# Two graph layers on one core: operations written in the order of their places, a new opening, and new places for the first and last graphs

## The chip, the cores and the metric

The kernel runs on one core of one Trainium2 chip. The metric is the device time of one execution in microseconds (us), as the median of several runs. The engines of the core are called PE (TensorE, matrix products; PEld is its loading of weights), DVE (VectorE), ACT (ScalarE), POOL (GpSimd) and SP (SyncE, which here only issues DMAs).

## The reference

There are 64 graphs of 256 nodes with 512 features each, and a weighted adjacency `adj` of 256 x 256 per graph. Two layers follow each other; each normalizes its input, applies a graph operation and adds the result to its input.

```python
# layer 0
h = jnp.maximum(_layernorm(x), 0.0)
deg = jnp.sum(adj, axis=-1, keepdims=True)
agg = jnp.einsum('bij,bjf->bif', adj, h) / jnp.maximum(deg, 1e-6)
x = x + relu(jnp.einsum('bnf,of->bno', jnp.concatenate([h, agg], axis=2), W))
# layer 1
h = jnp.maximum(_layernorm(x), 0.0)
Xw = h @ Wv + bv
sj, si = Xw @ aw[:512, 0], Xw @ aw[512:, 0]
e = leaky_relu(sj[:, None, :] + si[:, :, None] + ab[0], negative_slope=0.2)
alpha = adj * jnp.exp(e)
transition = alpha / (jnp.sum(alpha, axis=-1, keepdims=True) + 1e-12)
H, Xk = 0, h
for k in range(3):
    H = H + Xk @ Wk[k] + bk[k]
    Xk = jnp.einsum('bij,bjd->bid', transition, Xk)
x = x + relu(H)
```

## The kernel before

All products are float32. The kernel does fewer of them than the formula has: blocks of the two factors are added and subtracted first, so that seven block products do the work of eight (and 26 those of 32 for `W`), and the results are combined while they come out of PSUM. The sums of left and right factors are made by POOL and DVE, PSUM is emptied by ACT and DVE, and PE multiplies. PSUM has eight banks, `bank[0]` to `bank[7]`.

**Stages of one graph.** `prepare` (layernorm, Relu, degree scaling), `wide` (the 26 products with W, from tables `EARLY` for graphs 0 and 1 and `STEPS` for the others), `layer0` (the product with the scaled adjacency, in `main`, and the residual in `finish`), `turn1` (second layernorm and the four row sums that give `sj` and `si`), `transition` (the softmax-like matrix), `moved`, `once` (transition times h), `inner` (what is multiplied by the transition a second time) and `outer` (the three terms summed, in `main` again, and the store). Several graphs are in flight at once: while `outer` of one graph runs, `wide` and `layer0` of the next ones fill its gaps.

**Turning matrices.** For most graphs a matrix is transposed by DVE in blocks of 32 (`put`), written to DRAM by four DMAs (`dh`, `dan`, `dtt`) and read back (`get`). The first graphs and the last two, where nothing hides the trip, are transposed by PE instead (`flip_on_pe`, tagged L404 in the profile). `sj` also goes through DRAM: one DMA writes it (`ds<-sj`), a second one (`row<-ds`) reads it back onto all partitions; `transition` then applies Prelu and Exp to it on ACT (L692, L695), weights it with the adjacency on DVE (L697), scales it on ACT (L703, `an`) and has it transposed (`tt`).

**The weights.** At the start `weights_l0` loads the four half-megabyte blocks of W into the buffers of later x tiles (L784), PE transposes them in eight groups of four 128 x 128 blocks (L796), ACT copies them out, and DVE forms the right-hand sums from them (28 operations, L812 and L814). `weights_l1` does the same for the second layer's weights.

**What sets the order.** Nothing is scheduled automatically. `Plan.add` records each operation with its engine, its reads and writes and a *place*: a number from the table `AT`, plus the graph's number times `TURN`. `Plan.emit` sorts the operations of each engine by place; that is the engine's order in the program. It then writes the engines' queues into one program, so that nothing is written ahead of what it depends on: engine by engine, as far along each queue as possible. The tables whose names end in `_0`, `_1`, `_2` hold the places of graphs 0 to 2, those in `_late` and `_last` those of graphs 62 and 63, and `first` and `weights` those of the opening; the other tables serve all graphs between.

**DMA semaphores.** DMAs take eight completion semaphores in turn, in the order in which they are written into the program, and an issue waits until the previous user of its semaphore has landed. So at most eight DMAs are in flight, and SP, which issues in order, stands still at the ninth until the first has landed.

**Names that the change touches.** `first` (the opening loads), `warm` (dummy products; `WARM` is 0 before, so there are none), `main` with its branch `last` for graph 63 (banks `p, r, d` and two spare banks 6 and 7), `AT`, and the ACT costs in `norm_relu` and `scaled`, which are only noted, not executed. In `main`, steps 5, 1, 6 and 7 accumulate one after the other in bank `p`; after each, DVE adds a seed to what stands there into another bank, on which steps 2, 3 and 4 continue.

Of the kernel before, what the change touches and what calls it, by code (L numbers as in the profile page):

```python
# [15 lines left out]
P = 128  # L16
# [8 lines left out]
WARM = 0  # L25
TURN = 38.52
AT = {
    "first": (-90.93, -53.23, -117.99, -108.94, -110.36, -116.23, -69.23, -51.75, -160.39, -107.21, -61.21, -22.37, -27.53, -12.34, -45.26, -1.78,
        -84.29, -28.27, -93.32, 13.37, -47.15, -20.43, -156.60, -71.50, -119.21, -46.84, -42.27, -129.45, -122.63, -61.71, -52.35, -32.94, -72.67,
        -62.56, -45.91, -151.57, -67.52, -60.72, 2.83, 15.02, -11.78, 19.40, 29.16, -47.95, -25.77, 48.23, -47.81, -32.81, -19.46, -48.89, 7.13,  # L30
        20.41, -32.63, 17.85, 10.53, -123.51, 5.76, 21.86),
    "inner": (105.13, 108.59, 106.23, 109.69, 109.89, 110.76, 112.05, 116.38, 111.97, 114.07, 117.47, 117.50, 122.79, 115.08, 117.06, 118.02, 137.51),
    "inner_0": (104.64, 107.10, 112.63, 109.63, 108.85, 109.21, 114.17, 115.99, 113.73, 110.41, 129.80, 114.72, 119.54, 110.75, 113.34, 116.02,
        129.11),
    "inner_1": (110.70, 112.22, 111.49, 112.47, 113.83, 115.31, 114.08, 115.66, 116.33, 115.18, 129.29, 117.74, 125.91, 116.89, 117.80, 117.56,
        155.03),
    "inner_2": (110.70, 111.20, 111.98, 113.63, 111.78, 114.32, 114.94, 116.88, 115.46, 116.06, 116.42, 116.98, 124.86, 117.74, 119.04, 117.57,
        134.35),
    "inner_last": (336.53, 367.29, 384.59, 334.45, 391.73, 454.67, 522.64, 533.37, 408.60, 470.37, 504.02, 528.93, 492.30, 558.54, 500.07, 537.12,
        580.23),  # L40
    "inner_late": (108.31, 111.76, 110.85, 113.85, 112.13, 112.69, 114.05, 114.68, 123.33, 115.61, 145.82, 118.27, 122.89, 115.88, 119.11, 120.04,
        164.89),
    "layer0": (20.96, 24.01, 34.26, 38.15, 36.30, 37.47, 38.90, 39.56, 40.20, 40.90, 41.49, 42.16, 41.93, 42.79, 43.22, 43.47, 44.25),
    "layer0_0": (43.30, 43.73, 40.76, 63.15, 62.04, 64.91, 63.69, 65.17, 65.45, 66.86, 68.03, 68.37, 68.31, 69.19, 69.32, 68.45, 68.75),
    "layer0_1": (31.27, 36.57, 33.97, 43.43, 46.13, 48.74, 46.62, 49.21, 46.86, 49.66, 48.01, 49.83, 48.25, 48.79, 50.67, 49.93, 50.78),
    "layer0_2": (24.88, 28.19, 23.22, 43.47, 37.98, 37.09, 39.47, 39.22, 40.19, 41.59, 40.57, 42.04, 42.75, 43.10, 41.23, 47.00, 44.33),
    "layer0_last": (50.01, 57.68, 33.91, 60.79, 65.66, 66.71, 68.41, 66.94, 69.01, 68.24, 69.91, 69.27, 70.80, 71.03, 72.73, 71.96, 75.23),
    "layer0_late": (15.20, 21.71, 35.30, 40.31, 42.84, 48.47, 47.89, 49.57, 47.98, 49.76, 48.90, 49.94, 48.91, 50.48, 49.70, 51.70, 50.97),
    "loads": (-59.49, -45.29),
    "loads_2": (-40.12, -36.06),  # L50
    "loads_last": (-58.91, -32.90),
    "loads_late": (-54.89, -85.13),
    "moved": (89.04, 92.46, 93.17, 93.66, 94.15, 98.50),
    "moved_0": (94.08, 96.00, 97.15, 96.58),
    "moved_1": (87.63, 93.34, 94.62, 96.56, 97.69, 105.10),
    "moved_2": (88.68, 91.56, 91.23, 91.84, 96.02, 106.19),
    "moved_last": (139.05, 163.46, 205.96, 169.91),
    "moved_late": (96.66, 97.72, 100.63, 101.15),
    "once": (61.25, 64.00, 75.09, 75.88, 94.29, 95.59, 94.96, 99.41, 98.19, 98.63, 100.80, 101.23, 101.56, 100.30, 105.75, 103.00, 102.97, 103.89,
        106.56, 107.35, 108.14),  # L60
    "once_0": (85.34, 86.38, 98.69, 87.50, 93.62, 98.46, 98.58, 97.73, 98.58, 100.34, 100.69, 102.20, 101.36, 98.56, 103.24, 103.33, 102.27, 102.98,
        104.33, 105.25, 108.42),
    "once_1": (57.59, 69.48, 97.24, 96.50, 95.31, 95.58, 95.01, 99.66, 97.26, 98.27, 100.29, 102.15, 100.46, 102.80, 103.34, 105.40, 106.15, 108.95,
        105.21, 110.88, 111.17),
    "once_2": (63.41, 76.25, 69.81, 96.68, 93.52, 97.13, 93.09, 100.30, 100.95, 102.43, 103.05, 103.30, 102.21, 102.90, 103.59, 109.13, 104.57,
        107.39, 107.54, 109.97, 115.46),
    "once_last": (102.80, 135.83, 148.28, 162.89, 124.41, 120.18, 145.98, 187.50, 162.35, 203.89, 212.10, 233.57, 187.89, 213.05, 223.02, 232.11,
        256.18, 243.42, 255.25, 267.18, 321.27),
    "once_late": (66.99, 88.23, 64.29, 90.92, 99.96, 101.37, 100.45, 101.19, 101.37, 101.90, 105.80, 107.13, 110.31, 103.81, 110.60, 107.37, 105.93,
        106.50, 106.70, 107.63, 115.35),  # L70
    "outer": (108.93, 110.52, 122.87, 129.37, 114.22, 117.68, 119.41, 120.07, 120.70, 121.57, 122.87, 123.53, 124.60, 125.46, 126.33, 126.99, 127.62,
        130.65, 131.52, 132.19, 128.92, 131.95, 134.55, 134.99, 141.93, 152.31, 138.02, 140.19, 162.69, 160.60, 164.14, 164.93),
    "outer_0": (94.35, 98.74, 125.62, 106.70, 102.31, 116.27, 117.12, 118.24, 117.50, 117.80, 121.31, 124.46, 124.00, 125.58, 126.52, 126.71, 128.22,
        128.87, 132.65, 133.67, 128.80, 131.21, 134.36, 137.61, 140.55, 144.44, 136.33, 141.49, 160.49, 160.36, 163.66, 166.03),
    "outer_1": (106.89, 111.90, 118.77, 120.53, 108.75, 117.68, 119.18, 119.21, 120.59, 120.95, 123.23, 122.93, 123.75, 126.63, 126.70, 127.43,
        127.87, 128.74, 130.19, 132.33, 130.44, 131.84, 139.05, 141.13, 148.79, 152.10, 133.45, 136.68, 160.29, 160.80, 164.22, 166.72),
    "outer_2": (108.39, 111.96, 127.91, 140.81, 108.40, 121.23, 123.19, 121.63, 124.71, 125.64, 126.27, 125.65, 128.28, 128.68, 129.01, 128.91,
        131.04, 134.92, 135.36, 134.36, 132.23, 135.69, 137.94, 142.17, 143.69, 152.32, 138.41, 140.22, 150.30, 161.80, 164.00, 171.57),
    "outer_last": (498.02, 668.57, 694.33, 671.17, 577.46, 581.61, 593.26, 565.87, 615.19, 623.17, 650.49, 630.60, 695.13, 726.44, 735.87, 784.68,
        743.01, 838.42, 843.34, 796.04, 842.17, 761.60, 792.50, 751.08, 788.70, 811.00, 818.37, 858.45, 840.44, 876.17, 953.80, 975.74, 975.14,  # L80
        1020.56, 876.63, 891.60, 907.44, 875.80, 872.80),
    "outer_late": (109.06, 117.31, 186.73, 151.51, 116.15, 116.30, 119.62, 120.47, 120.01, 120.90, 123.12, 123.38, 129.10, 132.52, 132.66, 129.78,
        134.77, 139.77, 140.44, 139.50, 141.87, 144.49, 145.13, 158.57, 188.07, 200.85, 150.49, 152.04, 158.47, 232.29, 199.18, 211.96),
    "prepare": (-43.06, -41.74, -40.72, -35.30, -36.24, -28.72, -27.19, -23.45, -19.80, -15.93, -24.36, -24.98, -20.94, -12.75, -1.76, -2.28, -14.82,
        -13.49, -12.68, -12.13, -11.03, -11.58, -0.32, 1.04, 0.48, 2.14, 1.59),
    "prepare_0": (-84.88, -53.30, -37.93, -28.72, -22.39, -78.13, -74.85, -6.63, -18.20, -7.49, -144.71, -60.68, -137.04, -101.76, -12.58, -21.22,
        -26.38, -2.11, -10.47, 18.05),
    "prepare_1": (-15.07, -17.62, -8.06, -6.13, -0.14, -1.19, -0.63, 0.54, 7.75, 18.63, -38.44, -18.61, -14.54, 4.73, 16.46, 7.28, 12.55, 17.02,
        21.02, 19.33),
    "prepare_2": (-29.75, -29.48, -28.24, -24.75, -27.62, -28.40, -18.19, -16.40, -14.88, -13.91, -13.33, -6.35, -3.17, 8.62, 7.51, 7.67, -7.58,  # L90
        -2.32, -3.08, -1.25, 10.97, -0.12, 9.45, 9.24, 6.13),
    "prepare_last": (-41.49, -47.42, -40.82, -36.74, -38.40, -39.37, -36.21, -27.41, -24.96, -22.93, -7.95, -5.29, -3.53, 0.52, -2.38, -0.41, -8.95,
        -8.06, 0.10, 9.16, 6.05, -3.83, 2.64, 1.68, 2.00, -1.88, -3.02),
    "prepare_late": (-34.61, -47.32, -24.01, -19.75, -22.44, -22.19, -20.22, -19.93, -12.10, -16.22, -28.31, -35.76, -26.99, -25.62, -0.63, -19.64,
        -11.10, -13.45, -13.43, -9.03, -11.19, -7.53, -0.35, -0.68, -1.43, -1.97, 0.33),
    "prepared": (-7.18, 5.89, 11.28),
    "prepared_0": (8.94, 11.22, 28.01, 44.28),
    "prepared_1": (30.89, 31.47, 31.46, 30.86),
    "prepared_2": (13.00, 25.59),
    "prepared_last": (9.25, 6.90, 2.69),  # L100
    "prepared_late": (-3.13, 0.63, 10.23),
    "transition": (52.39, 56.28, 64.51, 63.42, 65.05, 63.97, 66.52, 67.12, 67.73, 68.04, 68.40, 68.92, 69.51, 71.25, 71.80, 70.70, 72.35),
    "transition_0": (74.09, 74.94, 85.61, 86.74, 87.55, 87.22, 90.49, 90.24, 90.60, 91.41, 91.25, 92.03, 91.61, 91.53, 93.51, 94.10),
    "transition_1": (53.67, 62.32, 65.20, 65.85, 69.15, 70.70, 67.77, 67.85, 67.92, 69.48, 74.55, 74.24, 70.13, 70.67, 70.52, 71.81, 77.46),
    "transition_2": (50.97, 58.93, 62.74, 64.48, 64.38, 64.92, 66.27, 66.53, 66.87, 67.29, 67.28, 69.70, 68.73, 73.40, 72.79, 67.23, 74.57),
    "transition_last": (75.67, 87.14, 127.84, 118.12, 129.35, 119.80, 108.57, 101.56, 114.50, 118.16, 130.61, 133.55, 117.50, 129.78, 119.38, 136.82),
# [165 lines left out]
def gnn_two_layers(ctx: ExitStack, tc: tile.TileContext, x, adj, w0, wv, bv, aw, ab, wk, bk, out):  # L272
# [628 lines left out]
    def first():  # L901
# [7 lines left out]
        weights_l0()  # L909
        load(0, "a")  # L910
        load(1, "x")
        load(1, "a")

    def warm():

# [60 lines left out]
```

## Time and profile before

| | before |
|---|---|
| median of 3 runs | 2546.91 us (2546.01 to 2550.6) |
| the profiled execution's own time | 2545.75 us |
| its span in the profile | 2544.0 us |
| granted TensorE clock, mean | 0.997 |
| PE busy | 2509.1 us (99%) |
| PEld, DVE, ACT, POOL busy | 2213.5, 1653.6, 1322.6, 1560.1 us |
| bytes moved | 296.85 MB, mean 117 GB/s |

The span is what the instruction records cover; the execution's own time is 1.75 us longer. PE's busy share counts a matrix product as busy from its start to its modelled end, at whatever clock it ran, so "busy" does not mean "at full speed". A float32 product of 128 x 128 by 128 x 256 has two records, a transpose of a 128 x 128 block has one. In the timeline, a row merges equal instructions that follow each other: start, time covered, engine, line, operation, tile written, tile read, shapes, count, and in brackets the idle time ahead of it with what ended that.

### The profile page before, as it was taken

The page shows a single profiled execution, that of the slowest core. Times are in us where ns is not written, and L with a number is a line of the kernel's source. Part 1 is how long each engine was busy: PE and PEld are TensorE (multiplying, and loading weights), DVE is VectorE, ACT ScalarE, POOL GpSimd, SP SyncE. Part 2 cuts the span into 40 slices and gives each one's busy share as a digit, 9 for nine tenths or more (in the row PEclk, how much of TensorE's full clock was granted, in tenths as well). Part 3 has the DMA queues.
Part 4 walks back from the last instruction along what each step waited for, and adds up shares of the span by engine and source line. Part 5 has one row for each costly group of instructions (what it writes and reads, how often), then busy time and mean ns, then how long its engine had stood idle before and what let it go on. Part 6 is the DMA issues. An engine that isn't in the chain of part 4 may idle for free.

```text
span 2544.0 us, 39950 instructions
## 1 busy us (share of the span) xinstructions
PE 2509.1 (99%) x12412; PEld 2213.5 (87%) x12412; DVE 1653.6 (65%) x4099; ACT 1322.6 (52%) x3551; POOL 1560.1 (61%) x2475
## 2 busy tenths in 40 slices
PE   7899999999999999999999999999999999999998
PEld 5688888888888888888888888888888888888887
DVE  5766666666666666666666666666666666666654
ACT  7455555555555555555555555555555555555521
POOL 5565666666666666666666656656666666666640
PEclk9999999999999999999999999999999999999999
DMA  4354454454454454444444544544544544544421
GB/s 150 85 131 117 113 129 120 115 125 117 117 129 112 115 135 110 119 125 120 120 120 116 127 121 111 128 122 113 127 119 117 126 113 116 135 112 115 110 71 44
DMA packets 574571, 296.85 MB, mean 117 GB/s; under 512 B 417171, under 2 KB 540819, under 8 KB 574358
## 3 DMA queue, kind: packets, MB, share of 16 engines
q1 hardware_dynamic: 574358, 294.31, 47.0%
q8 instruction: 98, 1.61, 0.3%
q14 instruction: 115, 0.94, 0.1%
HBM read 162.80 MB, written 131.40 MB: 116 GB/s over the span
## 4 chain that ended last, share of the span: by engine, by line
PE 96%; DVE 1%; DMA 1%; SPq 0%; ACT 0%; issue 0%; POOL 0%; DVEq 0%; ACTq 0%; POOLq 0%
PE bank L459 96%; DMA dh<-turned 0%; DMA x<-in_L_gnn_W_dram 0%; DMA l<-in_L_gnn_Wv_dram 0%; SPq L380 0%; DVE bank L474 0%; DVE zg L420 0%; DMA out_dram<-x 0%; DVE z L677 0%; DVE turned L376 0%; PE bank L404 0%; ACT h1n L362 0%; DVE bank L652 0%; SPq L345 0%; DVE zg L474 0%
## 5 line engine op out<-in xcount | busy, mean ns | idle before, releaser
L459 PE MATMUL bank<-l,s 128*128 128x256 f32 x3292 | 876.9, 380 | 6.6 <-ACT bank L546 2.1
L459 PEld LDWEIGHTS bank<-l,s 128*128 128x128 f32 x3292 | 611.6, 191 | 91.4 <-issue 5.1
L471 ACT COPY stg<-bank 128x256 f32<-128x256 f32 x944 | 337.2, 371 | 524.8 <-PE bank L459 203.6
L459 PE MATMUL bank<-l,zg 128*128 128x256 f32 x1820 | 469.2, 380 | 1.6 <-ACT mz L471 0.9
L459 PE MATMUL bank<-lq,zg 128*128 128x256 f32 x1792 | 447.8, 380 | 3.7 <-DVE zg L474 1.3
L459 PEld LDWEIGHTS bank<-lq,zg 128*128 128x128 f32 x1792 | 340.4, 190 | 51.1 <-DVE zg L474 2.3
L459 PEld LDWEIGHTS bank<-l,zg 128*128 128x128 f32 x1820 | 337.2, 191 | 42.3 <-ACT mz L471 1.7
L422 POOL TENSOR_TENSOR zg<-zg 128x256 f32<-128x256 f32 x183 | 131.7, 733 | 353.8 <-ACT zg L471 347.4
L652 DVE TENSOR_TENSOR bank<-bank,stg 128x256 f32<-128x256 f32 x505 | 210.3, 428 | 202.1 <-PE bank L459 138.8
L459 PE MATMUL bank<-l,h0t 128*128 128x256 f32 x1008 | 291.3, 382 | 1.6 <-DVE q L652 0.8
L422 POOL TENSOR_TENSOR s<-h0t,s 128x256 f32<-128x256 f32 x315 | 234.0, 743 | 0.5
L459 PEld LDWEIGHTS bank<-l,h0t 128*128 128x128 f32 x1008 | 197.4, 197 | 26.8 <-DVE q L652 2.3
L677 DVE SCALAR_TENSOR_TENSOR z<-h1n,v_sb 128x512 f32<-128x512 f32 x256 | 211.9, 828 | 13.1 <-ACT h1n L368 4.4
L459 PE MATMUL bank<-l,h1t 128*128 128x256 f32 x784 | 203.3, 381 | 1.3 <-DVE lo L477 1.0
L471 ACT COPY qf<-bank 128x256 f32<-128x256 f32 x128 | 47.6, 372 | 285.3 <-DVE qf L474 250.3
L422 POOL TENSOR_TENSOR qf<-qf 128x256 f32<-128x256 f32 x122 | 113.5, 930 | 117.4 <-DVE qf L474 117.4
L459 PEld LDWEIGHTS bank<-l,h1t 128*128 128x128 f32 x784 | 153.1, 197 | 20.1 <-DVE lo L477 2.3
L563 DVE SCALAR_TENSOR_TENSOR x<-bank,x 128x512 f32<-128x512 f32 x254 | 165.4, 686 | 2.7 <-PE bank L459 1.9
L459 PE MATMUL bank<-q,sa 128*128 128x256 f32 x512 | 152.9, 380 | 2.3 <-DVE bank L474 1.6
L459 PE MATMUL bank<-qf,st 128*128 128x256 f32 x512 | 152.6, 380 | 0.8 <-DVE qf L420 0.7
L422 POOL TENSOR_TENSOR s<-h0t 128x256 f32<-128x256 f32 x189 | 143.5, 773 | 9.3 <-ACT h0t L410 6.6
L422 POOL TENSOR_TENSOR hf<-h1n,hf 128x256 f32<-128x256 f32 x124 | 91.3, 736 | 89.9 <-PE bank L459 89.9
(178 smaller groups left out, 4418.3 us busy)
## 6 DMA issues: line engine op xcount, KB each, us to landing
dh<-turned SPq DMA_DIRECT2D x500, 128.0 KB, 3.3
h1t<-dh SPq DMA_DIRECT2D x64, 512.0 KB, 3.8
x<-in_x_dram SPq DMA_DIRECT2D x63, 512.0 KB, 4.6
out_dram<-x SPq DMA_DIRECT2D x63, 512.0 KB, 3.1
h0t<-dh SPq DMA_DIRECT2D x61, 512.0 KB, 4.0
a<-in_adj_dram SPq DMA_DIRECT2D x64, 256.0 KB, 4.3
dan<-turneda SPq DMA_DIRECT2D x248, 64.0 KB, 1.9
raw<-dan SPq DMA_DIRECT2D x62, 256.0 KB, 2.7
```

Of the source, the lines that this page charges most:

```text
L422: add("POOL", cost, lambda: getattr(nc.gpsimd, f)(to, p, q), reads, writes)
L459: nc.tensor.matmul(ps, lhs, rhs, start=start, stop=True, skip_group_check=True)
L471: add("ACT", 0.37, lambda: nc.scalar.copy(dst, bank[b][:, cols]), [f"bank{b}"], dkeys)
L563: add("DVE", 0.75 if sums else 0.69, lambda c=c: nc.vector.scalar_tensor_tensor(t[:, c, :], bank[banks[1 + c]], 0.0, t[:, c, :], op0=ALU.m ...
L652: add("DVE", 0.43, lambda f=f, to=to, x=x, y=y: getattr(nc.vector, f)(to, x, y), pbk + [k], tok)
L677: add("DVE", 0.79, lambda s=s, c=c: nc.vector.scalar_tensor_tensor(scr.rearrange("p c n -> p (c n)"), h[:, c, :], 1.0, v_sb[:, s, :], op0= ...
```

## The change

1. **Emission.** `emit` writes, of all operations that are ready, the one with the smallest place, one at a time; before, it took engine after engine. Each engine's own order is still the order of its places.
2. **The opening.** The two halves of graph 0's x are issued by ACT, not by SP. Seven groups of four products of the identity with itself go to PE (28 in all, into bank 2): five groups ahead of W0's first blocks and two between its third and fourth group. SP's first issues become: x of graph 1, the four W blocks, adj of graph 0, then bk, adj of graphs 2 and 1 and the weights of layer 1. Before they were: a W block, adj of graph 0, a W block, half of x, a W block, the other half of x, the last W block, then the weights of layer 1.
3. **The last graph.** In the `last` branch of `main`, step 6's sum goes straight to `bank[7]`, where step 3 continues; before it went to the upper half of `bank[r]`, from where ACT copied it to `bank[7]`. That copy (L546) is gone.
4. **Places.** New tables for the opening, for graphs 0 to 2 and for graphs 62 and 63. In the tables of the graphs between, a single number changes (a copy in `inner`, 117.47 to 117.62), which changes no engine's order.
5. Three noted costs of ACT instructions change; no instruction does.

In the two programs' instruction lists, PE's order is the same, and every instruction waits for the same instructions, from about the 520th to the 5910th of PE's some 6270 instructions, and over the matching stretch on the other engines. What differs lies ahead of and behind that: in the profile before, up to about 115 us and from about 2400 us.

```diff
-WARM = 0
+WARM = 7
 AT = {
+    "warm": (-428.00, -428.00, -428.00, -428.00, -428.00, -302.00, -302.00),
...
@@ Plan.emit
-            for e, queue in queues.items():
-                while heads[e] < len(queue) and self.ops[queue[heads[e]]][2] <= done:
-                    i = queue[heads[e]]
-                    self.ops[i][1]()
-                    done.add(i)
-                    heads[e] += 1
-                    left -= 1
+            ready = [(self.ops[q[heads[e]]][3], e) for e, q in queues.items() if heads[e] < len(q) and self.ops[q[heads[e]]][2] <= done]
+            if ready:
+                e = min(ready)[1]
+                i = queues[e][heads[e]]
+                self.ops[i][1]()
+                done.add(i)
+                heads[e] += 1
+                left -= 1
...
@@ main
         p, r, d = banks[:3]
+        e, cols = (banks[4], lo) if last else (r, hi)
...
-        plus(bank[r][:, hi], [f"bank{r}"], p, lo, s12, keys[1:])
+        plus(bank[e][:, cols], [f"bank{e}"], p, lo, s12, keys[1:])
         step(7, p, lo, terms)
         if last:
-            x, y = banks[3:]
+            x = banks[3]
             plus(bank[x][:, lo], [f"bank{x}"], p, lo, s21[:, 1], keys[1:])
             last(1, hi, x, lo)
             plus(bank[d][:, lo], [f"bank{d}"], p, lo, s21[:, 0], keys[:1])
             step(2, r, lo, terms)
-            add("ACT", 0.37, lambda: nc.scalar.copy(bank[y][:, lo], bank[r][:, hi]), [f"bank{r}"], [f"bank{y}"])
             last(0, lo, r, lo)
-            step(3, y, lo, terms)
-            last(0, hi, y, lo)
+            step(3, e, cols, terms)
+            last(0, hi, e, cols)
             step(4, d, lo, terms)
             last(1, lo, d, lo)
...
@@ warm, first
+    def warm():
+        for _ in range(WARM):
+            def run():
+                for k in range(FC):
+                    nc.tensor.matmul(bank[2][:, k * P : (k + 1) * P], ident, ident, start=True, stop=True, skip_group_check=True)
+            add("PE", 0.86, run, ["ident"], ["bank2"])
...
         for c in range(NC):
-            add("SP", 0.8, lambda c=c: nc.sync.dma_start(t[:, c, :], x[0, c * P : (c + 1) * P, :]), [], [f"{k}.{c}"], 3.0, port=256)
+            add("ACT", 0.1, lambda c=c: nc.scalar.dma_start(t[:, c, :], x[0, c * P : (c + 1) * P, :]), [], [f"{k}.{c}"], 3.0)
...
+        kept = plan.count
+        plan.stage("warm")
+        warm()
+        plan.stage("first")
+        plan.count = kept
         weights_l0()
         load(0, "a")
         load(1, "x")
         load(1, "a")
```

## The prediction

> **What bounds the kernel now.** The page first: busy shares (first line) and the forty slices.
>
> ```profile
> PE 2509.1 (99%) x12412; PEld 2213.5 (87%) x12412; DVE 1653.6 (65%) x4099; ACT 1322.6 (52%) x3551; POOL 1560.1 (61%) x2475
> ...
> PE   7899999999999999999999999999999999999998
> ```
>
> PE is the bound; only the outer slices have gaps. Second, the windows by stage (span, time, busy time of PE, PEld, DVE, ACT, POOL, then granted clock, DMA share, GB/s).
>
> ```profile
> 0.00:20.00 20.00, 9.95 (x45) 8.29 (x46) 7.35 (x23) 12.97 (x37) 3.13 (x14) 1.00 0.95 314
> 60.00:80.00 20.00, 14.65 (x59) 9.89 (x57) 14.15 (x35) 13.05 (x38) 15.70 (x25) 0.95 0.33 60
> 80.00:100.00 20.00, 15.23 (x66) 11.79 (x65) 14.34 (x38) 9.10 (x25) 9.74 (x13) 0.80 0.48 112
> 600.00:1000.00 400.00, 400.00 (x1990) 356.31 (x1989) 262.13 (x649) 211.68 (x570) 257.74 (x409) 1.00 0.49 120
> 2520.00:2544.00 24.00, 16.92 (x66) 13.09 (x65) 4.41 (x11) 0.73 (x2) 0.00 (x0) 0.93 0.07 22
> ```
>
> From 600 to 1000 us PE never waits. The instruction lists agree there, so **the change acts only at head and tail**. Idle understates their loss, because PE also runs slowly after gaps. So I count the *excess*: elapsed time less PE's records at their mid-run price (0.2165 us for 128x256, 0.109 for 128x128). It is 15.4 us by 20.6, 19.5 by 41, 27.0 by 70, 38.6 by 91.5, 44.0 by 113, then flat. At the end, idle is 2.7 us in 2400–2520 and 7.1 in 2520–2544, the last store's flight included.
>
> Third, the chain of waits: 96% PE, with W's DMAs, `dh` and a few DVE and ACT lines in the rest. So I went to the timelines of head and tail.
>
> **What the skill says.** "TensorE: Matmul & The Clock Gate", Part 1: PE starts at half clock, gets the full one after some 3.4 us of sustained work and loses it after an idle window as long. The trace agrees in kind: opening transposes take 4.32/19 = 0.227 us against 0.109 later, and after gaps four 128x256 records take 1.92 us, not 1.03. "DMA: Bandwidth & Descriptors", section "Issuing engines are not separate DMA queues": DMAs of ACT and SP share the same 16 engines; a second issuer saves only issue time. Agreed so far as the trace goes: DMA share 0.95 in the first 20 us, an SP issue about 0.43. "ScalarE: Activation LUTs", "What ACT_TABLE_LOAD costs", puts it at 1283 ns; the trace has 1.28.
>
> **Part 1, the opening: -1.9 (bounds -3.5 and +4.8).** PE's timeline (start, time covered, operation, tiles, count, idle before):
>
> ```profile
> 4.35 0.45 PE L796 MATMUL bank<-ident,x 128*128 128x128 f32 x1 [4.35 <-DMA x<-in_L_gnn_W_dram]
> 7.14 2.82 PE L796 MATMUL bank<-ident,x 128*128 128x128 f32 x12 [2.34 <-DMA x<-in_L_gnn_W_dram]
> 11.08 4.32 PE L796 MATMUL bank<-ident,x 128*128 128x128 f32 x19 [1.12 <-DMA x<-in_L_gnn_W_dram]
> ```
>
> PE waits for W, and each transpose runs at half clock. Landings, from the waits: W blocks at 4.32, 7.1, about 9 and 11.03. Issue order gives 0.52 MB by 4.32 and 2.88 by 11.03: 2.36/6.71 = 0.35 MB/us. Queued ahead of W's end after: x of graphs 0 and 1, then W: 2.1 MB by the second block, (2.10-0.52)/0.35 + 4.32 = 8.8 us; 3.15 MB by the last, 11.8. adj of graph 0, second before, lands at about 12.5, not 4.98: its sum on ACT (0.61, L573) now holds the Relu of `h0n` behind it, and DVE's degree operations stand ahead of the sums of W. ACT's two issues (0.43 each) come ahead of its table load (1.28), which then ends near 2.9, before x lands. Wv's second half, on whose landing (19.54) the first W products waited, lands near 18.8.
>
> The 28 unit products have two records each: 0.45 us cold, 0.22 warm (twice the transposes above). Twenty fit ahead of 8.8 us: cold 9 us from 1.3, so up to 10.3. If they bring the full clock, 16 transposes after the last landing take 16 x 0.109 = 1.75, end 13.5 against 15.40 before: **-1.9**. If all stays cold, 28 x 0.45 + 32 x 0.225 = 19.8 from about 0.4 after the identity: ends at 20.2, **+4.8**. I take the warm case: these are plain products, 20 in a row for over 3.4 us. The gain is kept only if `h0n` and the 28 DVE sums (0.34 each, to 25.7 before) move forward as well; -3.5 if Wv's earlier half helps too.
>
> **Part 2, transition of graph 0: -5.5 (bounds 0 and -8.5).** SP's issues, two ACT rows, then PE's:
>
> ```profile
> 57.78 0.35 SPq L686 DMA_DIRECT2D ds<-sj  x1
> 63.50 0.35 SPq L380 DMA_DIRECT2D dh<-turned  x1
> 63.94 0.44 SPq L687 DMA_DIRECT2D row<-ds  x1
> ```
>
> ```profile
> 74.76 0.72 ACT L362 ACTIVATE h1n<-x,sm 128x512 f32<-128x512 f32 x1
> 76.99 0.49 ACT L703 ACTIVATE an<-z,tot 128x256 f32<-128x256 f32 x1
> ```
>
> ```profile
> 77.53 0.44 PE L404 MATMUL bank<-ident,an 128*128 128x128 f32 x2 [0.74 <-ACT an L703]
> 79.62 0.69 PE L404 MATMUL bank<-ident,an 128*128 128x128 f32 x2 [1.65 <-ACT an L703]
> 80.77 1.22 PE L459 MATMUL bank<-tt,h1n 128*128 128x128 f32 x4 [0.46 <-ACT tt L410]
> 81.78 1.92 PE L459 MATMUL bank<-l,s 128*128 128x256 f32 x4
> 85.31 1.19 PE L459 MATMUL bank<-l,s 128*128 128x256 f32 x2 [1.61 <-ACT stg L471]
> ```
>
> `sj` leaves at 57.78, but its read-back is issued 6 us later, behind a `dh` write that waits for DVE. Prelu starts at 68.77, DVE's L697 at 74.41 behind layer 0 of graph 1, and the two `an` scalings come at 76.99 and 79.08 among graph 1's norm (L362, L570, L368). PE has meanwhile run out of layer 0, and flips and products with `tt` follow one by one. From 74.9 to 88.0, 13.1 us pass for 3.5 us of work: 1.04+0.74+1.65+0.46+1.61 = 5.5 idle, the remaining 4.1 slow records.
>
> After: `row` follows `ds` on SP, the two row totals of L700 stand among the additions of layer 0, both `an` stand ahead of graph 1's norm on ACT (some 2.4 us sooner for the first, 4 for the second), and W products of graph 1 and 2 stand between the products with `lq`, `tt` and `st`. I estimate that the 5.5 idle goes and that slow records stay at other, new gaps; all of 1.65+1.04+1.61+slow 4.1 = 8.5 is the far bound, nothing the near one. Next late would be `h1t`, back from DRAM (POOL waits for it 9.55 us at 89.2), and POOL's sums with `hf`. What is moved behind: graph 1's norm, by two `an` (1 us), hidden by W products.
>
> **Part 3, the rest of the ramp: 0 (bounds -5 and +3).** 41–70 lost 7.5 us, 88–113 about 6. Every table of graphs 0 to 2 is new, SP and POOL queues too; no view prices this, so I take nothing: 2 us of `dh` queueing either way is plausible. Issue counts stay, but for two moved to ACT.
>
> **Part 4, the tail: -4.2 (bounds -2.1 and -4.6).** All engines:
>
> ```profile
> 2532.44 0.76 DVE L474 TENSOR_TENSOR bank<-bank,lo 128x256 f32<-128x256 f32 x2 [4.74 <-PE bank L459]
> 2533.24 0.75 DVE L756 SCALAR_TENSOR_TENSOR x<-bank,x 128x256 f32<-128x256 f32 x2
> ...
> 2534.08 0.36 ACT L546 COPY bank<-bank 128x256 f32<-128x256 f32 x1 [13.70 <-DVE x L756]
> ...
> 2534.49 1.13 PE L459 MATMUL bank<-l,s 128*128 128x256 f32 x4 [2.09 <-ACT bank L546]
> ```
>
> Step 7 ends in bank `p`, DVE adds, ACT copies, PE stands 2.09 us, then does 20 records in 6.29 us that cost 4.33 at full clock. After, step 7 precedes step 2, whose 10 records (2.17 us) cover DVE's three operations (0.42+0.34+0.34), and step 3 reads bank 7 directly. From step 7's start, 2527.85, PE has 40 records: 40 x 0.2165 = 8.66, end 2536.5 against 2540.76: **-4.2**. If the clock still drops: 2.09 alone, -2.1. Behind it one DVE operation and the store stay, 3.2 us. Earlier in graphs 62 and 63 flips have fewer fillers: 0 (±0.6).
>
> **Part 5, emission and noted costs: 0.** Waits and order between are identical; at the edges it only decides which queue takes which semaphore, in part 3's bounds.
>
> Sum: -1.9 - 5.5 + 0 - 4.2 = **-11.6**. Against the profiled execution's own 2545.75: 2534.15. The median shown lies 1.16 higher, so **2535.3**.
>
> **Rivals.**
> - A, the sum holds: 0.52.
> - B, the ramp gives part 2 back: DRAM trips of `h1t` (over 9 us of POOL's waiting) set graph 0's pace whatever the transition does. -6.1, 2541: 0.20. For: seven of eight stages wait on them. Against: W products can fill.
> - C, the ramp gains in full (part 2 -8.5, part 3 -3): -17.6, 2529: 0.12.
> - D, the change does not warm: the clock ignores the unit products, +4.8 for -1.9; with the others -4.9, 2542: 0.06. For: the early clock column reads 1.00 while transposes ran cold, so it is no witness.
> - E, slower: Prelu (L692) now stands early in ACT's in-order queue. `row` took 4.83 us, 63.94 to 68.77; ACT's PSUM copies stand behind Prelu, and PE stalls when no bank is free. It decides if `row` lands over about 3 us after Prelu's place; then 3–6 us of stall per graph, doubled by the clock, at graphs 0 and 1: +18 against -11.6, so +6, 2553: 0.10.
>
> **How the numbers follow.** A measurement can tell 0.2% (5.1 us) from none. A and C are faster almost wholly, B for 0.6 of it, D for half: 0.51+0.12+0.12+0.03 = 0.78. Within 0.2%: rest of A, B and D, 0.12; E 0.10. The range, 2527 to 2544, holds A, B, D and most of C, and leaves out E and C's far end. Its ends stand for -20 and -3.
>
> **What would show it.** Right: opening transposes near 0.11 us and W0 done by 14; `row` issued within 1 us of `ds`; no idle over 1 us between 70 and 90, and PE excess 36 or less by 113; the tail's PE gap gone, PE's end 3.2 us ahead of the last landing. Wrong: PE waiting on `h1t`, `row` or Prelu in the 40–110 windows, or transposes at 0.225 until 20 us.

## The result, and the profile after

The changed kernel takes 2534.65 us (2533.68 to 2535.09), before in the same comparison 2548.26 (2546.01 to 2550.6): ratio 0.9946, 95% interval 0.9933 to 0.9959. The forecast was 2535.3, range 2527 to 2544. By these medians 13.6 us are gained; the profiled executions differ by 11.3. The profiled execution took 2534.47 us, its span is 2532.7 (before 2545.75 and 2544.0).

The page again, busy shares and slices: PE has 99% as before, and only its first slices differ.

```profile
PE 2505.8 (99%) x12468; PEld 2212.1 (87%) x12468; DVE 1646.5 (65%) x4099; ACT 1322.9 (52%) x3550; POOL 1562.3 (62%) x2475
...
PE   8899999999999999999999999999999999999998
```

The windows of head and tail (same columns as before; the last one is again the last 24 us of the span):

```profile
0.00:20.00 20.00, 13.65 (x96) 12.96 (x97) 6.38 (x20) 10.88 (x31) 2.04 (x11) 0.95 0.93 328
60.00:80.00 20.00, 15.61 (x71) 10.98 (x70) 17.00 (x48) 15.39 (x45) 14.59 (x25) 1.00 0.30 56
80.00:100.00 20.00, 17.36 (x84) 13.84 (x83) 14.06 (x42) 11.04 (x31) 12.50 (x17) 1.00 0.75 181
2508.70:2532.70 24.00, 18.84 (x84) 15.41 (x82) 6.03 (x15) 0.74 (x2) 2.63 (x4) 1.00 0.07 23
```

PE does 84 records in 80–100 us where it did 66, at clock 1.00 where it was 0.80, and 84 in the last 24 us where it did 66. The first window's 96 records contain the 56 of the unit products, so there is no gain to be read from it.

Both traces have PE's records in full, so record n of before (counted from 0) can be set beside record n + 56 of after. How much earlier PE starts the same ordinal:

| record of before (its time) | after earlier by, us |
|---|---|
| 50th (21.5 us) | -0.8 |
| 100th (31.6) | -1.6 |
| 200th (55.7) | 0.0 |
| 250th (72.1) | 2.0 |
| 300th (90.3) | 8.0 |
| 350th (105.4) | 9.9 |
| 450th (127.5) | 7.1 |
| 1100th to 11700th (258 to 2386) | 7.9 |
| 12380th (2529.65) | 7.4 |
| 12411th, the last (2540.4) | 11.5 |

Up to the 933rd record (224 us in before, not only the 115 us given with the change) and from the 11709th (2388 us) the orders of the two kernels differ, so an ordinal there isn't always the same product, and the split between neighbouring lines is rough; between the two it is the same product. So the opening gives nothing by itself, the stretch of graph 0's transition (250th to 300th) gives 6.0 of the head's 7.9 us, nothing happens for 2100 us, and the last 31 records give 4.0.

The stretch 78 to 88 us shows what kind of gain it was. Before, then after:

```profile
78.00:88.20 10.20, 6.51 (x21) 5.06 (x22) 8.01 (x21) 3.94 (x9) 1.68 (x3) 0.50 0.36 100
```

```profile
78.00:88.20 10.20, 8.78 (x49) 7.35 (x50) 7.16 (x22) 4.87 (x14) 5.60 (x7) 1.00 0.55 121
```

The clock column is 0.50 against 1.00: PE ran the whole 10.2 us at half clock before and at full clock after. Its 6.51 us of records would have taken about half of that by the estimate that every record halves, so some 3.3 us went to the clock alone, beside the idle time. In the whole trace of before half clock stands for 17.1 us (3.4 from 19.9, 10.2 from 78.0, 3.4 from 2535.6), in that of after for 3.4 (from 17.9); the cold start of the opening, where the column reads 1.00, is not in these sums. As half clock can cost at most half of its length, these stretches explain at most 6.9 of the 11.5 us by which PE's last record comes earlier.

### The profile page after: what moved, and what is told of

Same layout as the page of the kernel before. It is cut to its first block, busy times and chain, and to the rows that moved or that the text cites. A ratio compares the mean times of both kernels' runs of the same rounds, so it can differ in the third digit from the quotient of the medians.

```text
span 2532.7 us, 40078 instructions
## 1 busy us (share of the span) xinstructions
PE 2505.8 (99%) x12468; PEld 2212.1 (87%) x12468; DVE 1646.5 (65%) x4099; ACT 1322.9 (52%) x3550; POOL 1562.3 (62%) x2475
## 4 chain that ended last, share of the span: by engine, by line
PE 96%; POOL 1%; DMA 1%; DVE 1%; ACT 1%; issue 0%; SPq 0%; DVEq 0%; POOLq 0%; ACTq 0%
PE bank L462 95%; DMA dtt<-turneda 0%; POOL s L425 0%; DMA x<-in_L_gnn_W_dram 0%; DMA raw<-dtt 0%; DMA raw<-dan 0%; POOL zg L425 0%; PE bank L799 0%; POOL sa L425 0%; POOL hf L425 0%; PE bank L407 0%; DVE bank L477 0%; ACT h1n L365 0%; ACT h1n L371 0%; POOL q L425 0%
```

## Experiments: head, tail, and a stall that had two keys

Each line of the table was timed in five rounds (tail_only, copy_gone, row_early and emit_inner in 11 to 21 executions); "before" is the kernel before in the same comparison. The changed kernel was timed in the first comparison alone. An interval is some 0.13% either way (3.3 us) where before and variant have only those rounds, so differences of 1 to 3 us between variants are read from their traces, by the same alignment of records as above, and not from the medians alone. The profiled execution of before, 2545.75 us, is some 1 to 2 us faster than its medians here, so gains read against its trace are on the small side.

| kernel | us | before, us | ratio (95%) |
|---|---|---|---|
| head_only | 2533.13 | 2547.85 | 0.9942 (0.9929–0.9954) |
| tail_only | 2545.81 | 2547.85 | 0.9991 (0.9983–0.9999) |
| no_warm | 2533.49 | 2547.85 | 0.9945 (0.9931–0.9958) |
| copy_gone | 2544.60 | 2547.85 | 0.9987 (0.9981–0.9994) |
| emit_only | 2562.04 | 2547.34 | 1.0061 (1.0049–1.0074) |
| emit_inner | 2541.50 | 2547.66 | 0.9975 (0.9966–0.9984) |
| row_late | 2537.32 | 2547.34 | 0.9960 (0.9947–0.9972) |
| row_early | 2547.85 | 2547.34 | 1.0001 (0.9993–1.0010) |
| an_late | 2536.48 | 2547.34 | 0.9961 (0.9947–0.9974) |
| undo_trans | 2537.51 | 2546.83 | 0.9966 (0.9952–0.9979) |
| x_on_sp | 2536.24 | 2547.66 | 0.9956 (0.9943–0.9968) |
| opening2 | 2531.15 | 2547.66 | 0.9938 (0.9924–0.9951) |

**head_only**: the changed kernel with before's tables of graphs 62 and 63 and before's `last` branch.

```diff
-    "outer_last", "inner_late", ... : of the changed kernel
+    "outer_last", "inner_late", ... : of before (all names in _last and _late)
-            e, cols = (banks[4], lo) if last else (r, hi)
+            add("ACT", 0.37, lambda: nc.scalar.copy(bank[y][:, lo], bank[r][:, hi]), ...)
```

> The changed kernel with the tail of before: tables of graphs 62 and 63 and the last branch of main with its copy. Theory 1 (the two ends are independent, since the stretch between waits for nothing): the gain of the head alone, 7.7 us by the alignment of the two traces at PE's middle records, so about 3.6 us slower than the changed kernel. Theory 2 (the head's gain is only a shift that the tail's loads and DMAs use): clearly less than 7 us, and head and tail alone do not add up to the whole.

Both theories fell: with the old tail the kernel was not slower than the changed one, and by its trace 1.7 us faster. Its last 31 records gain 4.0 us although the copy is there. The reason stands in its tail, all engines:

```profile
2521.79 1.03 PE L412 MATMUL bank<-l,zg 128*128 128x256 f32 x4
2522.04 0.36 ACT L499 COPY bank<-bank 128x256 f32<-128x256 f32 x1 [12.07 <-PE bank L412]
...
2523.09 1.03 PE L412 MATMUL bank<-l,s 128*128 128x256 f32 x4
2523.29 0.76 DVE L427 TENSOR_TENSOR bank<-bank,lo 128x256 f32<-128x256 f32 x2 [4.74 <-PE bank L412]
```

The copy (L499 here) starts under the products of step 7 and waits for PE alone. In before it started behind DVE's `x` addition (its bracket, shown above, says so), though it needs nothing from that. Both only read the same bank. The tail's new places, on the other hand, cost: from the 11700th to the 12380th record the changed kernel loses 0.5 us where this one gains 0.8.

**tail_only**: before with the other kernel's tail.

```diff
+    all tables in _last and _late, and the branch last of main, from the changed kernel
```

> Before with the tail of the changed kernel: its tables for graphs 62 and 63 and its last branch without the copy; the head and the emission are those of before. Theory 1: 3.6 us faster than before (4.0 in the last graph, 0.4 lost ahead of it), PE's gap of 2.09 us ahead of step 3 gone. Theory 2 (the tail gains only when the head has shifted it): under 2 us.

Before with this tail is 2.0 us faster by the medians. In its trace the last 31 records gain 4.05 us, and the stretch ahead of them (11700th to 12380th) loses 1.1. So theory 1 holds for the stall, and the loss ahead of it was under-sized at 0.4.

**copy_gone**: before with edit 3 alone, and with no other place changed.

```diff
+        e, cols = (banks[4], lo) if last else (r, hi)
-        plus(bank[r][:, hi], [f"bank{r}"], p, lo, s12, keys[1:])
+        plus(bank[e][:, cols], [f"bank{e}"], p, lo, s12, keys[1:])
...
-            add("ACT", 0.37, lambda: nc.scalar.copy(bank[y][:, lo], bank[r][:, hi]), [f"bank{r}"], [f"bank{y}"])
```

> Before with one edit: in the last branch step 6's sum goes straight to bank 7 and the copy L546 is gone; order and places as before, so step 2 still stands in the middle of step 7. Theory 1 (the copy alone is the stall, since step 3 follows step 7 and has its seed long before): the 2.09 us of idle PE go and the clock holds, 3.5 to 4.1 us faster than before, as much as the whole tail. Theory 2 (as the prediction had it, step 2 behind step 7 is what covers DVE's additions): PE still waits, for DVE's additions now, and only about 1 to 2 us are won.

3.25 us faster; the last 31 records gain 4.05. Theory 1: the copy was the whole stall, and step 2 still stands in the middle of step 7. The new order of steps isn't needed.

**emit_only**: before with the new emission alone.

```diff
-            for e, queue in queues.items():
-                while heads[e] < len(queue) and ...
+            ready = [(self.ops[q[heads[e]]][3], e) for e, q in queues.items() if ...]
```

> Before with the new emission alone: same operations, same places, same order on every engine. Theory 1 (the prediction's part 5): nothing, within 1 us of before, and ACT's copy L546 still starts behind DVE's two x additions. Theory 2 (the order in which instructions are written decides what an instruction waits for: the copy, now written ahead of DVE's x addition that reads the same bank, no longer waits for it, as the run with the head alone showed): the copy starts some 2 us sooner, under PE's last products of step 7, the gap of 2.09 us is gone, and the whole is 3 to 4 us faster; the head is unchanged.

Neither theory: it is 14.7 us **slower**. The last 31 records do gain 4.05 us, as theory 2 said, but by the 11700th record it has lost 20.7, in nearly equal parts over the whole middle, where nothing had been expected. Around 654 us, ACT, DVE and PE:

```profile
653.94 0.37 ACT L472 COPY qf<-bank 128x256 f32<-128x256 f32 x1 [3.73 <-PE bank L460]
```

```profile
654.42 0.42 DVE L475 TENSOR_TENSOR qf<-bank,qf 128x256 f32<-128x256 f32 x1 [0.58 <-ACT qf L472]
654.76 0.42 DVE L475 TENSOR_TENSOR bank<-bank,p 128x256 f32<-128x256 f32 x1
```

```profile
654.18 1.03 PE L460 MATMUL bank<-l,zg 128*128 128x256 f32 x4
655.33 0.67 PE L460 MATMUL bank<-q,sa 128*128 128x256 f32 x2
```

and the same place in before, ACT, DVE and PE:

```profile
650.82 0.37 ACT L471 COPY qf<-bank 128x256 f32<-128x256 f32 x1 [4.26 <-DVE qf L474]
```

```profile
650.36 0.42 DVE L474 TENSOR_TENSOR qf<-bank,qf 128x256 f32<-128x256 f32 x1 [0.18 <-PE bank L459]
```

```profile
650.52 1.03 PE L459 MATMUL bank<-l,zg 128*128 128x256 f32 x4
651.38 0.59 PE L459 MATMUL bank<-q,sa 128*128 128x256 f32 x2
```

In before ACT waits for DVE, which hurts nobody: PE's next product follows 0.86 us after the four (650.52 to 651.38), without a gap. With the new emission DVE waits 0.58 us for ACT, its next addition into a bank comes late, and PE stands still for 0.29 us (between 654.18 + 4 x 0.2165 = 655.04 and 655.33). That comes back every 38.5 us, once per graph, and is most of the 0.36 us that each of some 57 graphs loses. Over the whole trace DVE waits 59 times for this copy, 35.5 us together; in before it never does.

The Trainium skill has the reason in "PSUM — Partial Sum Buffer", section "PSUM bank collisions raise a hardware error": two engines that access one bank at the same time collide, reads against reads included, and so the compiler's scheduler adds a dependency between any two instructions of different engines on one bank. The traces agree in that one of the two readers waits for the other, here and in the last graph; that it is this dependency is inferred from it. Which one waits, the runs say: the one that is written later into the program. In these tables the copy has place 117.47 and DVE's sum 117.50.

**emit_inner**: the same with one number.

```diff
     "inner": (105.13, 108.59, 106.23, 109.69, 109.89, 110.76, 112.05, 116.38, 111.97, 114.07,
-        117.47, 117.50, ...
+        117.62, 117.50, ...
```

> Before with the new emission and one place: in the tables of the graphs between, inner's copy goes from 117.47 to 117.62, so behind DVE's sum of the same bank (117.50). Theory 1 (ACT's copy and DVE's sum only read that bank, but the one written later waits for the one written first; at 117.47 the copy is written first and DVE waits, 0.29 us of PE for each of some 57 graphs): the 15 us of the run with the emission alone are gone, DVE's sum comes first again, and what is left is the last graph's copy, 3 to 4 us faster than before. Theory 2 (the emission costs through other waits as well): still slower than before, or no faster than it.

Theory 1, and somewhat more: 6.2 us faster than before. By its trace 4.05 of it are the last 31 records, 0.4 lie in the head and 0.8 in the late graphs; the rest of the median's 6.2 is a matter of which executions were profiled (2545.75 of before, whose median here is 2547.66; 2540.53 of this one). The 20.7 us of the middle are gone. So **the number that changes no engine's order is worth some 20 us** under the new emission: with the tables of the graphs between as they are, edit 1 can't be had without it.

## Experiments: the opening

What PE did there after the change:

```profile
1.35 6.09 PE L909 MATMUL bank<-ident 128*128 128x128 f32 x40 [1.35 <-POOL ident masks.py:199]
8.62 1.53 PE L799 MATMUL bank<-ident,x 128*128 128x128 f32 x12 [1.17 <-DMA x<-in_L_gnn_W_dram]
9.98 1.95 PE L909 MATMUL bank<-ident 128*128 128x128 f32 x16
11.77 1.91 PE L799 MATMUL bank<-ident,x 128*128 128x128 f32 x16
13.51 0.60 PE L407 MATMUL bank<-ident,h0n 128*128 128x128 f32 x4
13.95 0.60 PE L799 MATMUL bank<-ident,x 128*128 128x128 f32 x4
18.37 2.08 PE L462 MATMUL bank<-l,h0t 128*128 128x256 f32 x4 [3.82 <-ACT h0t L413]
```

The transposes are fast (16 in 1.91 us, 0.12 each) and W is done at 14.55 us. Then PE is idle for 3.82 us, drops to half clock (3.4 us from 17.9), and its first four records of W take 2.08 us. What was won by 14.55 is gone.

**no_warm**: the 28 unit products left out, all places kept.

```diff
-WARM = 7
+WARM = 0
```

> The changed kernel without the 28 unit products, all places kept. Theory 1 (the full clock that they bring is what the opening gains): transposes of W at 0.225 us instead of 0.109, W done at about 16.5 us instead of 14.5, and 2 to 3 us lost by the end. Theory 2 (the sums of W on DVE set the pace, and PE's transposes have slack, as the 3.8 us of idle PE after them says): transposes just as slow, but the first W product comes within 1 us of where it was, and the whole changes by under 1 us.

```profile
8.62 6.19 PE L748 MATMUL bank<-ident,x 128*128 128x128 f32 x28 [8.62 <-DMA x<-in_L_gnn_W_dram]
14.62 0.63 PE L356 MATMUL bank<-ident,h0n 128*128 128x128 f32 x4
15.08 0.60 PE L748 MATMUL bank<-ident,x 128*128 128x128 f32 x4
18.36 2.07 PE L411 MATMUL bank<-l,h0t 128*128 128x256 f32 x4 [2.68 <-ACT h0t L362]
```

Theory 2: the transposes are cold again and W ends 1.1 us later, but the first product starts at 18.36 against 18.37. The unit products do what they say and bring nothing in this order of work.

**x_on_sp**: x of graph 0 issued by SP, first in its queue.

```diff
-            add("ACT", 0.1, lambda c=c: nc.scalar.dma_start(t[:, c, :], x[0, ...]), ...)
+            add("SP", 0.8, lambda c=c: nc.sync.dma_start(t[:, c, :], x[0, ...]), ...)
```

> The changed kernel with graph 0's two x halves issued by SP, first in its queue, instead of ACT. Theory 1 (only issue time is saved, and the opening is paced by DVE's sums of W): x lands about as before, the W blocks about 0.9 us later (two issues of 0.43), under 1 us slower by 20 us and under 1 us in all. Theory 2 (early x is what lets the opening start): the first W product over 1 us later and 1 to 2 us lost.

Theory 2's size for the opposite reason. x landed 2.7 us *earlier* (its sum starts at 4.17 us instead of 6.83), and W 2.0 us *later*:

```profile
10.64 1.53 PE L799 MATMUL bank<-ident,x 128*128 128x128 f32 x12 [2.06 <-DMA x<-in_L_gnn_W_dram]
...
20.43 2.08 PE L462 MATMUL bank<-l,h0t 128*128 128x256 f32 x4 [3.86 <-ACT h0t L413]
```

The first product comes 2.06 us later and the 2.0 us stay to the end of the head (its middle records are 1.96 us behind the changed kernel's). The opening hangs on W. Of W's 2.0 us, 0.9 is SP's issuing (its four W issues start at 2.10 instead of 1.22); that from ACT's queue x shares the engines with W instead of standing ahead of it is the likely rest, and not tested apart.

**opening2**: head_only with ten places moved.

```diff
 # ACT
-  L573 x2 (adj of graph 0), Relu h0n[0], copy l0.5, L573, ..., Relu h0n[1], ..., copy h0t
+  Relu h0n[0], copy l0.5, ..., Relu h0n[1], copy h0t, copy l0.11, ..., L573 x2
 # DVE: the two operations on deg behind 17 sums of W
```

> The kernel with the changed head and the tail of before, with ten places of the opening moved: on ACT the two sums of adj of graph 0 (L573, which wait for its landing at 11.9 us) go behind the copies of W and the Relus of h0n, the copy that DVE's first sum of W waits for goes ahead of them, the copy of h0t goes directly behind its flip; on DVE the two degree operations go behind 17 sums. Theory 1 (ACT's order holds both the sums of W and the first W product): DVE's first sum at 12.7 us instead of 13.4, the first W product at about 16.2 instead of 18.4, and 1 to 2 us are kept. Theory 2 (the gain is taken back by the sums of W on DVE, which run without a gap to 24 us): within 0.5 us of the run without it.

```profile
14.12 0.60 PE L753 MATMUL bank<-ident,x 128*128 128x128 f32 x4
16.45 0.68 PE L416 MATMUL bank<-l,h0t 128*128 128x256 f32 x2 [1.73 <-ACT zg L428]
17.31 0.68 PE L416 MATMUL bank<-l,h0t 128*128 128x256 f32 x2 [0.18 <-DVE l L771]
```

Theory 1: the first product at 16.45 instead of head_only's 18.12, idle 1.73 instead of 3.85, and no half clock behind it, nor anywhere in this trace's clock column (head_only's has 6.8 us of it from 16.8). DVE's first sum came at 12.98 against head_only's 13.19, less than expected. The middle records are 2.6 us ahead of head_only's; by the medians, each against its own before, the gain is 1.8. At 2531.15 us (2530.08 to 2532.14) this is the fastest kernel here; its interval still overlaps the changed kernel's.

## Experiments: graph 0's transition

SP, ACT and PE after the change:

```profile
57.38 0.34 SPq L689 DMA_DIRECT2D ds<-sj  x1
60.34 0.34 SPq L690 DMA_DIRECT2D row<-ds  x1
```

```profile
71.18 0.91 ACT L706 ACTIVATE an<-z,tot 128x256 f32<-128x256 f32 x2 [2.28 <-DVE tot L703]
```

```profile
74.46 0.44 PE L407 MATMUL bank<-ident,an 128*128 128x128 f32 x2 [0.69 <-DVE tt L413]
...
75.57 0.70 PE L462 MATMUL bank<-l,s 128*128 128x256 f32 x2 [0.24 <-ACT stg L474]
...
78.56 0.67 PE L462 MATMUL bank<-l,s 128*128 128x256 f32 x2 [1.41 <-ACT stg L474]
```

`row` is issued 3.6 us sooner than before and `an` comes 5.8 us sooner (71.18 against 76.99). Of the 5.5 us in which PE stood idle there, 2.3 are left. Four runs undo or add steps.

**row_late** (`row` behind the `dh` writes), on the changed kernel:

```diff
     "transition_0": (61.61,
-        65.18, ...
+        72.50, ...
```

> The changed kernel with one place moved: graph 0's read-back of sj (row) goes behind the four dh writes and one load on SP, as it stood before. Theory 1 (row's place on SP is what held graph 0's transition): row is issued at about 64.5 us instead of 60.3, Prelu 3 us later, PE's excess by 91 us is 3 to 5 us larger. Theory 2 (DVE's and ACT's places set it, SP had slack): Prelu moves by under 1 us or PE's fillers take it, under 1 us in all.

`row` is issued at 64.48, ACT waits 1.82 us for it, Prelu starts at 68.03 instead of 66.11, and 1.5 us are lost by the middle (2.7 by the medians, 3.6 with each against its own before; the profiled execution is the slowest of its five). By the trace row's place counts for about half of what theory 1 gave it; the medians lie at theory 1's lower end.

**row_early**, on before:

```diff
     "transition_0": (74.09,
-        74.94, ...
+        74.10, ...
```

> Before with one place moved: row goes directly behind ds on SP, ahead of the dh write. Theory 1 (row is what held the transition): Prelu comes some 3 us sooner and 2 to 4 us are won by 91 us. Theory 2 (the transition was held at several points in a row, and L697 on DVE and the two an scalings on ACT stay where they are): Prelu comes sooner, an does not, and nothing is won.

0.5 us slower by the medians, ratio 1.0001: nothing. ACT's rows of before, then of this run, show why:

```profile
67.95 0.91 ACT L575 ACTIVATE an<-a,deg 128x256 f32<-128x256 f32 x2 [0.53 <-DVE deg L573]
68.77 0.94 ACT L692 ACTIVATE z<-row,si 128x256 f32<-128x256 f32 x2
```

```profile
69.34 0.91 ACT L579 ACTIVATE an<-a,deg 128x256 f32<-128x256 f32 x2 [0.52 <-DVE deg L577]
70.16 0.93 ACT L696 ACTIVATE z<-row,si 128x256 f32<-128x256 f32 x2
```

Prelu (the `z<-row,si` rows) starts directly behind the scaling of a later graph's adjacency both times, with no wait for `row` ahead of it. So theory 2 holds in what it says of the gain, but Prelu did not come sooner either: in before ACT's own order held it, and `row` had slack. In the changed kernel Prelu stands ahead of such a scaling, and there a late `row` did make ACT wait (row_late).

**an_late** (both `an` behind graph 1's Squares), on the changed kernel:

```diff
     transition_0, two entries
-        86.36, 86.51
+        88.30, 88.40
```

> The changed kernel with two places moved: both an scalings of graph 0 go behind the two Squares of graph 1's norm on ACT. Theory 1 (ahead of the norm is what the transition needed): an 3 to 4 us later, PE's two flips wait for it, 3 to 5 us lost by 91 us. Theory 2 (W products of graph 2 between the flips cover it): under 1 us.

`an` at 75.84, 4.7 us later; PE waits 2.98 us at the flips and runs 3.4 us at half clock; 2.0 us are lost by the middle (1.8 by the medians, 2.8 with each against its own before), of which 0.7 were lost by the 250th record, ahead of the moved places. Again between the two.

**undo_trans**: both together, and DVE's L700 to L703 behind layer 0 of graph 1.

```diff
     transition_0
-  row 65.18; DVE 81.78, 83.07, 83.76, 84.73; an 86.36, 86.51
+  row 72.50; DVE 85.21, 85.22, 85.23, 85.24; an 88.30, 88.40
```

> The changed kernel with the three moves of part 2 taken back together: row behind the dh writes on SP, both an scalings behind the Squares of graph 1's norm on ACT, and DVE's weighting and totals (L700 to L703) behind layer 0 of graph 1. Theory 1 (these three are the step that the prediction sized at 5.5 us): 4.5 to 6 us slower than the changed kernel, an at about 77 us. Theory 2 (most of the gain there comes from the W products that now stand between the dependent products, and the three moves are worth what the single ones showed): 2 to 3 us slower.

2.9 us slower by the medians, 4.3 if each is taken against its own before. Its runs spread from 2533.94 to 2538.99, and the profiled one is the lowest of them:

```profile
75.22 0.44 PE L411 MATMUL bank<-ident,an 128*128 128x128 f32 x2 [2.98 <-ACT an L710]
```

PE waits 2.98 us there too, but in that execution no stretch at half clock follows, and up to the middle it even lies 0.9 us ahead of the changed kernel's. `an` came at 74.68, not at the 77 that theory 1 expected. So the medians put the three moves at 2.9 to 4.3 us, from theory 2's range to just short of theory 1's, and the one trace at nothing; the intervals of the two ratios overlap (0.9952–0.9979 here, 0.9933–0.9959 for the change), so the size isn't settled.

The records 250 to 300, of which the moves are part, gained 6.0 us in the changed kernel and still 4.4 in this one, so a good part came from elsewhere. The clock says where to look: all six traces with before's opening tables (before, tail_only, copy_gone, emit_only, emit_inner, row_early) have 10.2 us of half clock there, from between 78.0 and 82.2 us on, and none of the eight with the changed ones has it, this one included (an_late has 3.4 us from 76.0). That stretch was estimated above at 3.3 us, most of the 4.4. What keeps it away are likely the W products that now stand between the dependent ones; no run moved them back, so that is argued, not shown. The spread of these five executions goes in part with the clock too: its mean is 0.999 in the fastest (2533.94) and in the one at 2536.76, and 0.998, 0.998 and 0.997 in the three slower ones, where 0.001 is about 5 us at half clock. Where in the run they lost it is open.

## Why the prediction was right, step by step

The time came out within 0.7 us of the forecast, but of its five terms only parts 2 and 4 had the right size, part 2 with another split; part 1 brought nothing, part 3 brought the difference, and part 5 was wrong. That parts 1 and 3 cancel is luck, and so is some of the closeness in time: the forecast started from a median of 2546.91 and took off 11.6, while before came out at 2548.26 and the gain at 13.6.

- **Part 1, the opening, -1.9: measured +0.8 by the 50th record, +1.6 by the 100th.** What failed is the condition that the part itself named, that `h0n` and DVE's sums move forward as well. The clock did come (0.12 us a transpose), W's end was 14.55 for 13.5 foreseen (15.40 before), and adj's late landing held ACT for 1.18 us at 11.93, as written there; but `h0t` was copied only at 17.69, and no_warm shows the whole term to be slack.
- **Part 2, -5.5: the records 250 to 300 (72 to 90 us) gained 6.0.** The size holds, the split does not. The idle time was to go: 2.3 of its 5.5 us are left. The slow records were to stay: they went, since the clock stayed full through 78–88 us, some 3.3 us. Two errors of about equal size cancel there. The three moves named are worth 2.9 to 4.3 us on the medians, not clear of noise, so they are not shown to be what did it. One link was read wrongly: in before Prelu did not wait for `row` but for ACT's own queue (row_early).
- **Part 3, the rest of the ramp, 0: -3.4.** The records 100 to 250 gained 3.5 us and 300 to 350 another 1.9; 350 to 450 gave 2.8 back, and 0.8 came by the 1100th. It lies in the bounds of -5 and +3, and it makes up for part 1. No run took it apart, so its cause stays open; the emission is not it, since emit_inner gains only 0.4 in the head.
- **Part 4, the tail, -4.2: -4.0 in the last 31 records.** The size was right. Its reason was one of two that each suffice: the copy gone (copy_gone) or the copy written ahead of DVE's read (emit_inner). That step 2 stands behind step 7 wasn't needed. The earlier tail, sized 0 (±0.6), cost 0.5 here and 1.1 in tail_only.
- **Part 5, emission, 0: wrong.** "Waits and order between are identical" was true of the two kernels as they stand, and hid that two edits cancel: the emission alone costs 20.7 us there, the new number in `inner` takes that back. And at the edge it decides more than semaphores: by itself, with that number, it is worth the tail's 4.0.
- **The rivals.** B: after the change POOL waited for `h1t` 2.6 us, not 9.5; still, of the 9.9 us that PE was ahead at the 350th record, 2.8 were given back by the 450th. C: the two ramp terms gave 9.4 us (6.0 and 3.4), not its 11.5. D: the products do warm the clock, and in this order of work it doesn't matter (no_warm). E: `row` was there when Prelu's turn came; only with row late did ACT wait (1.82 us in row_late), and PE lost 1.5, not 6. The 4.83 us that E gave row's trip took in ACT's own queue: where ACT did wait for it, it was 3.55 (64.48 to 68.03).
- **The signs named.** Met: opening transposes near 0.11 us, the tail's gap gone, PE's end 3.4 us ahead of the last landing (2529.28 and 2532.7), the excess by 113 us 8.9 smaller than before's with the unit products' 6.1 counted in, so some 35 where the prediction counted 44.0, under the 36 allowed. Not met: W0 done at 14.55 and not by 14; `row` 3.0 us behind `ds` and not within 1, since it waits for `ds` to land; one idle of 1.41 us at 78.56.

The error on the emission did not reach the sum, because the tail's 4.0 was counted once, under the copy; that on the opening was made good by the rest of the ramp, by luck.

## What to carry to other kernels

An edit that leaves every engine's order alone can still cost or save: where two engines only read one PSUM bank, the one written later waited here, so look at which of the two has someone waiting behind it. A gap on PE is dear by what follows it, so price the half-clock stretch and not the gap alone; but its length did not decide here whether the clock fell: 3.4 us of half clock came behind 2.09 us of idle PE in before's tail and behind 2.98 in an_late, none behind 2.98 in undo_trans or 1.73 in opening2. And ask of work that was sped up what its result waits for next, before booking it: PE's faster transposes fed a queue on ACT that took the time back.

## What the runs showed of the hardware that was not expected

The same instructions in the same order do not start equally each time. copy_gone has before's head, and its PE is 2.7 us later by the 150th record; part of it is a half-clock stretch at 41 us in which PE was never idle by its records:

```profile
41.20:44.60 3.40, 3.40 (x11) 2.52 (x10) 2.47 (x7) 0.38 (x1) 0.00 (x0) 0.50 0.01 2
```

In the 3.4 us ahead of it (37.8 to 41.2) the records fill PE too, at full clock, so the prediction's reading that the clock goes after an idle window does not explain it. row_early, with the same opening, has such a stretch at 39.9 us, before's own trace has none.

The half-clock stretches inside these traces last 3.4, 6.8 or 10.2 us, multiples of 3.4, which agrees with the window of about 3.4 us that the Trainium skill states in "TensorE: Matmul & The Clock Gate", Part 1. Before's runs spread over 4.6 us in the first comparison, the changed kernel's over 1.4. So one profile of each kernel can't settle 2 us in such a ramp.
